# A four-layer graph network on one core: residual adds with row sums on VectorE, variances by ScalarE squares, and an order table that models the DMA queue

## The chip, the core and the metric

The kernel runs on one core of one Trainium2 chip. The core has five engines with an instruction list each: TensorE (PE, matrix products into PSUM), VectorE (DVE), ScalarE (ACT), GpSimd (POOL) and SyncE (SP, which issues DMAs). Each engine takes its instructions strictly in the order of its list and waits on semaphores for the others. DMAs are issued by SP, ACT or POOL and run by themselves. The metric is the device time of one execution in microseconds (us); smaller is better.

## What is computed

The input x holds 16 graphs of 1024 nodes with 256 features, adj is one 1024 x 1024 adjacency matrix. Four layers follow, each of the form x = x + layer(relu(layernorm(x))):

```
h = jnp.maximum(_layernorm(x, axis=-1), 0.0)
x = x + _L0_gnn_ref(h, adj, L0_gnn_W, L0_gnn_a)     # 1 head, leaky_relu 0.01, relu
h = jnp.maximum(_layernorm(x, axis=-1), 0.0)
x = x + _L1_gnn_ref(h, adj, L1_gnn_W, L1_gnn_a)     # 1 head, leaky_relu 0.2, elu
h = jnp.maximum(_layernorm(x, axis=-1), 0.0)
x = x + _L2_gnn_ref(h, adj, ...)                    # dot-product attention, 8 heads, feed-forward
h = jnp.maximum(_layernorm(x, axis=-1), 0.0)
x = x + _L3_gnn_ref(h, adj, L3_gnn_W, L3_gnn_a)     # 4 heads, leaky_relu 0.2, elu
```

Layers 0, 1 and 3 are graph attention: weights exp(leaky_relu(e_src + e_dst)), masked by adj and normalised by row, times the projected features. Layer 2 is masked dot-product attention, whose middle is

```
x = _layernorm(x + t, ln1_g, ln1_b)
h = jax.nn.relu(jnp.einsum('fnc,cd->fnd', x, w1) + b1)
f_out = jnp.einsum('fnd,dc->fnc', h, w2) + b2
x = _layernorm(x + f_out, ln2_g, ln2_b)
```

So each graph passes six layer norms: one at the entry of each layer and two inside layer 2. Everything is fp32.

## The kernel before

All work is cut into tiles of 128 nodes (8 per graph) by 256 features. A stage is one layer of one graph (64 stages). Stages of different layers and graphs overlap: after a start-up the list of stages repeats layer 2, layer 1, layer 3, layer 0 of neighbouring graphs, so that stages that need much PE run beside those that need much DVE or ACT.

The program is first laid out as a list of operations (`op`, line 790), each with an engine, an estimated cost, a rank, the operations that it follows and the buffers it takes and releases. `play` (line 924) then fixes the order: `forward` walks through model time with the costs and with a delay per engine (`DELAY`, line 752), and at each step `choose` takes, of the operations that could begin within 0.5 us, the one with the smallest number in a table, `RANKS` (line 47, three characters for an operation). The instructions are recorded in that order, which is the order of each engine's list. Neither the costs nor the ranks exist at run time: on the chip only the order, the buffers and the semaphores remain.

The parts that matter here:

- **Norms.** `stats_of` (line 1023): DVE's bn_stats and bn_aggr give mean and variance of a tile, POOL forms (variance + eps)^-0.5 in two instructions (L1034, L1035), with a third (L1037) for layer 2. `way_in` (line 1064) uses it at the entry of each layer, `feed_forward` and `finish` inside layer 2. The normalised tile is then transposed on PE (L1054), copied out by ACT (L1057), and projected on PE (L1061).
- **Layers 0 and 1.** `gat_item`: DVE forms masked weights p (L1318), PE multiplies them with the values (L1335). `gat_out`: reciprocal of the row sum, relu (and exp in layer 1) on ACT, then the residual add: on POOL in layer 0 (L1361), two instructions on DVE in layer 1 (L1372, L1373). The next layer's `way_in` follows tile by tile.
- **Layer 3.** `sources` transposes the source terms (L1250), stores them to DRAM as rows `kept` and loads them back spread over all partitions as `r`; `pair_weights` forms the weights on DVE (L1391); PE multiplies them (L1425) and sums them (L1449).
- **Layer 2.** `dot_item` works on items of 128 keys x 512 queries x 4 heads: scores on PE (L1545), exp on ACT in two halves (L1559), mask on DVE in two halves (L1567), values on PE (L1576). The row sums of the weights need only the sum over keys, so two items are first added by a DMA: `gather` (L1593), issued by POOL, adds the odd item's tile (1 MB) onto the even one's with an accumulating DMA. PE sums the result with four matmuls (L1605). A gather waits for the even item's values and both items' masks. There are 256 gathers, 16 for each graph.
- **Feed-forward.** `dot_out` adds the attention to the tile y on POOL (L1658); `feed_forward` normalises (L1044, L1045), multiplies by w1; `finish` multiplies by w2, adds to y on DVE (L1723), normalises again, adds y to x on POOL (L1738), and calls the next layer's `way_in`.

The planner's model gives the gather a cost of 1.0 on POOL and a fixed delay of 8.0 until its result is there.

Of the kernel before, what the change touches and what calls it, by code (L numbers as in the profile page):

```python
# [28 lines left out]
U8 = mybir.dt.uint8  # L29
# [18 lines left out]
    "##,#M5#IA#&O#H2#2l#M)#'c#Q(#H#$6p#MC#GP##q##c#%-#$X##s##0##U#$0#$,##P##X##Y##1#$-##{#$)#$]#$M#%I#$j#$N#%E#%K#%Y"  # L48
    "##%#%O#%}#&Y#&d#&l#&s#';#'B##W##9#oB##N##B#oP##Z##?##>##[##D#ny##a$7g##`##r##l#$##$$#$8#$*##u##z#$6#$=##}#$(#$;"
    "##b#$V$8-##_##y$8,##d##A$7y##g##o#$'#$u##2#$9#$7#$K#%*##*#$H##]#$.##3#$A##t##v#$E#$F#,;##x##6#$5$%$##'#Q.##T#K9"  # L50
    "#K.#(,#%W#'`#'U#$n#)s#'k#%U#(`##^#%7#$&#$%#$1#$2#$C#$G#$I#$L##<#$?#$[#$4##f#%@#%L#&2#$<#$Q##j#81##w#%D#%Z#%`#Nz"
    "#$Z#$`####$r#&1#%f#%k#$Y#$k#%4#>9#%A#%5#%r#%&#%M#${#%=#&##xD#%{#'u#%a#'q#(:#%z#'t#$i##h#$+#$d#$_#$h#$s#$e#$@#`+"
    "#%?#$>#&B#&%#,R#&Z#[=#%;#$O#$v##i##H#'H#%g#%J#%[#%0#%/#%,#&M$D{#$x#%>#%N#%h#b8$?s#&0#(3#&+#&.#%y#%u#&($4Z#&&#&6"
    "#%b#&$#&)#&'$B+#&_#))#&:#%p#Du#;z#<%#%V##n$H^#$b#$p$3b#$^#T>$3P#$m#%1##(#%T##O#%|##R#$}$GF##-#$U##4##8##K#%.##$"
    "##M#%:#$y#$t#$q##I#$z#%<#$W#%)#%8#=M#%6#%+##/##&##@#$g#$a#%w#-%#-##%R$&s##5$=J#%H#%]#3Q#%i#,V#/+#&5#$l#&h#:-#CG"
    "#:=#%d#$S#$|#%2#%c#%j#%m#&,#%t#$J#$w#%x$?=#%C#)*#%F#%B#%l#$o#&-#(U#%Q#'2#+6#%o#&/#0,$'e#'G#h`##p#0'#%^#&7$Gw##k"
    "#%v$Hv#&F$Ha#&N#'-#&A#&Q#&V#&S#lN#&m#&4#'3#'/#b##':#%q#&a#&*#(l#&w#&{#&z#&9#&<$Hw#%S#(R#y$#(S#'6#&;#&?#&^#lO#&G"
    "#Y}#'X#'0#&W#&I#%X#)D#(?#'+#R0#&[#&L#&P#'J#(+#&H#'1#&R#&|#',#'@#&p#'Q#'r#&k#'Y#&f#'C#(f#'.#'L#(8#(=#'N#&U#;v#;l"
    "$-[#&K#&=#&b#&E#&g#&j#&t#''#%s#&i#&o#(y#'9#(;#6F#(<#&n#'$#'8$H'#'a#'y$4|#'5#&]#')#'s#&}$Bt#'^$7k#'l#'?#'<$C2#'h"
    "#'K#'}#<K#%$#'o##.#(6##C#'W#%(#(%##e#'E#'4#'S#'m#'R#'I#(5#'w#'(#'>#'x#jJ#&y$=Z#<J$:z#'F#'O#'7#%G#{)#&v#'z#)V#>U"  # L60
    "#'n#'_#%n#(&#'p#?/#(0#'M#(.#&J#(/#'j#&`#rr#_c#(F#8j#(q#Mm#(M#Mo#(d#Mn#'&#'%#(##'Z#{g#(*#)a#&8##:#(2#(N#(E#/V#)I"
    "#(B#(A#(C#(4#)]$+r#,e#)M#([#i&#((#()#,t#i'#w/#)c#(t#I2#(J#(Y#]h#(K#(V#)F#(_#Ms#(u#KE$Ea#)-#(c#N+#)S#IC#)b#)`#)g"
    "#)U#(i#)d#*(#8?#(m#(|#).#jZ#)1#(a#)$#LT#)##(g#)u#jQ#)n#)0#*R#(k#)8#)@#)C#(j#(]#({#(@#)R#']#)E#(Z#(n#'{#'A#(^#)T"
    "#)>#)G#(P#)&#)5#)v#*&#'P#(G#(X#)y#'D#)L#*q#);#Lj#'|#(9#*3#*$#(D#*,#)K$I0#(O$I@$,q#*##)B#)i#*;#(H#*+#*4#+H#*E#)J"
    "#+L#*9#)A#s}#**#(1#+@#)O#)x#*7#*P#/`#*a#*A#*Z#*8#VE#)?#*D#*0#*y#*6#-0#)N#*_#*k#+k#*s#*C#*^#b($$C#)=#*c#)t#*v#J2"
    "#*[#(w#*w#+U#*I#*i#zG#'v$>>#B=#*]#*g$J:#,h$%D#W5#*n#*M#+<#*|$B<#++#*O#WG#+/#*J#.'#+G$J;#+M#+?#*f#z}#*t#a)#*r$?%"
    "#+A#+8#*j#*u$3:#*d#*p#+d#+a#*S#,U#+C#)+#*-#+`#)}#+&#*K#/?#+R#CO#+O#+P#*}#+[#*'$*M#+^#+S#-[#+X#+c#),#0>#)4#)9#,$"
    "#'*#,v#+N#,r#,W#-<#,N#[S#,x#,O#-:#+D#-A#-G#,B#,d#-(#,j#-;#,L#--#+z#-C#,z#'[#-6#,i#-D#/b#[@#-I#.^#-a$EU#.J#.%$;%"
    "#-}#+b#-j#g)#.:#.)$9j#.7#.?#+B#+F#-H#+(#,&#R+#,D#,%#^1#+#$(u$%|#+)#(Q#-Z#,|#)Y#Lh#*>#2n#+g#+J#*1#cw#)X#,T#+T#,g"
    "#.&#,y#,l#+3#*)#,Z#+e#(-#+>#cj#,'#(L#-2#,5#,)#g`#,6#,:#,4#+}#,##C(#,Q#($$1`#+Z#,9#,X$5H#*L#)W$1_#,Y#-s#,0#+o#,b"  # L70
    "#|5#*B#,}#+r#,s#,?#,@#,>#+u#,n#,8$5J$=r#,K#+]#-Q#+n#.,#-?#.;#,J#+j#+p$5Q#)P#.<$5K#,f#+i#,M#,G#)%#+{#,1#,H#rc#+l"
    "$5P#,3#,S#zA#):#,I$Ab#,c#,/$En#.4$02#*F#,`#,u#,7#-9#+V#-e#,*#-c#.=#-v#-^#-@#-o#-Y#+q#-3#-K#-n#-p#.I#+f#.H#JZ#kE"
    "#,m#.P#.U#,k#.T#-|#.o#/(#k3#.V#.Y#-r#.b#.d#/3#,[#.*#-U#.t#.g#.s#.]#/1#-E#.R#.w#.W#.v#.n#,P#+.#-L#,+#-h#ho#/f#/P"
    "#-5#.k#/O#,]#,-#/Q#0r#/K#/)#/^#8/#-t#8M#-x#-w#/W#-l#)f#(s#)l#)[#*l#+4#)m#*N#*m#)o#+'#%'#)e$<.#*.#)w#*:#*<$Eg$,p"
    "#it#*`#*T#(x#*b#*U#(z$GW#)r#*/#*%#)z#(I#*Y#){#,(#)Q#)|#+I#*e#(>#)Z#*V#*X#)<#*x#*h#W6#+%#+7#`p#+*#+5#`s#+-#+9#^*"
    "#+0$%f#*=#.N#-'#-&#-)#+y#-,#-1#,a#-/#-4#-7#-]#z6#-J$;&#,_#-f#-d#.D#-$#-P#&C$;5#+:#.6#+=#-`#-i#-q#.3#J[#/d#0y#0U"
    "#.M#rQ#B3#.@#-B#,o#.K#,{#0n#._#?V#-g#-z#/t#,.#.9#.e#.G#/Y#.E#.h#/>#-k#./#.L#-F#.+#.8#.A#-X#.C#/0#-=#-{#/'#8-#.["
# [281 lines left out]
    "$Fz$IH$J-$HT$Ib$79#Ul$I?$J5$I+$G|$Iu#hA$EL$Hp$HW$H?$GV$I/$.{$HD#`j$Ig$H_$H:$78#<0#V>$J.$Hs$Ho$Du$HG#GJ$I.$Hu$H|"  # L359
    "#1Z$3G$Hf$HS#_;$HL$Hg$IW#('#y'#<E#xi$I_$J*#M{$J#$I1$J1$GR$I|#<x$II$GO$I($IS#WD$IX$Ia$IV$I]$IB#UX#UW$IT$@<$Im$I="  # L360
    "#q^$IG$IU$IQ$Id$IO#^r$IM#>M$Iz$HI$2d$CB#>e$Iy#yW$It$I}#p4#TS$J?$0R#pU$IZ$Ie$Ij$HN$I:$J@$Hq$Hm$Ih$IP$IL$Ip$I$#:["
    "$I,$IN#5e$I'$If$IY#Y&$Hy#m_$J6#%P$J%#jY$Il#k;#al$J8#wr$I{$J'$J9$Ir$I>"
)


# [1585 lines left out]
```

## Time and profile before

| | |
|---|---|
| Three runs | 4347.82, 4347.32, 4344.05 us; median 4347.32 |
| Profiled execution | 4346.76 us, of which the span from first to last instruction 4344.9 us |
| Mean granted PE clock | 0.983 of full speed |
| Gathers (POOL's DMA queue) | 268.45 MB, 30.7% of the 16 DMA engines' time |
| Exponentials of layer 2, L1559 on ACT | 1024, 1023 ns each |
| Masks of layer 2, L1567 on DVE | 1024, 1233 ns each |
| bn_stats on x, L1030 on DVE | 512, 415 ns each |
| Normalising activation, L1107 on ACT | 256, 505 ns each |
| POOL adds L1361, L1738, L1658 | 128 of 787, 128 of 920, 64 of 1413 ns |
| POOL's root, L1034 and L1035 | 768 of 367 and 768 of 736 ns |

A row of the profile's groups reads: line, engine, operation, output <- inputs by the program's names, their shapes, count, then busy time in us, the mean of one in ns, the idle time of the engine in front of them, and what ended it. A row of waits reads: engine, output and line <- what it waited for: total us, times, longest. Rows of windows give for a stretch of time the busy time of each engine (with its number of instructions), the granted PE clock, the share of the DMA engines and GB/s.

### The profile page before, as it was taken

How to read it: one execution, taken by the hardware profiler on the slowest of the kernel's cores; microseconds unless marked ns; L12 is line 12 of the kernel's file. 1: busy time of each engine (PE TensorE's matmuls, PEld its weight loads, DVE VectorE, ACT ScalarE, POOL GpSimd, SP SyncE). 2: the span in 40 equal slices, each digit the busy share in tenths (PEclk: the TensorE clock that was granted, in tenths of full speed). 3: DMA queues.
4: the chain of work that ended last, by engine and by line, in shares of the span. 5: the costliest groups of instructions: out<-in, count | busy, mean ns of one | idle time of the engine just before them, and what ended most of it. 6: DMA issues, size and time to landing. Idle time of an engine off the chain costs nothing. (4 is left out here: it accounts for less than half of the span.)

```text
span 4344.9 us, 66664 instructions
## 1 busy us (share of the span) xinstructions
PE 4143.8 (95%) x25993; PEld 2175.8 (50%) x25993; DVE 3368.5 (78%) x5836; ACT 2004.2 (46%) x3083; POOL 1408.4 (32%) x2281
## 2 busy tenths in 40 slices
PE   8999999998999999999999999998999999899988
PEld 7735264553645535455354554535545355464433
DVE  7578877878777788777878778777787877858788
ACT  4462635435354453634536354363543635455442
POOL 3323242423324233242322424224242241434231
PEclk9999999999999999999999999999999999999999
DMA  3061805317053170531606235162350713435261
GB/s 111 17 142 32 169 27 117 69 50 155 25 119 79 40 148 26 129 71 46 140 26 141 59 75 111 37 130 59 74 112 33 150 42 89 96 75 111 64 122 41
DMA packets 96451, 364.29 MB, mean 84 GB/s; under 512 B 10376, under 2 KB 45568, under 8 KB 63360
## 3 DMA queue, kind: packets, MB, share of 16 engines
q0 software_dynamic: 36864, 268.45, 30.7%
q1 hardware_dynamic: 58848, 90.98, 6.2%
q8 instruction: 206, 3.38, 0.3%
q14 instruction: 117, 0.96, 0.1%
q10 hardware_dynamic: 416, 0.52, 0.0%
HBM read 74.32 MB, written 17.17 MB: 21 GB/s over the span
## 5 line engine op out<-in xcount | busy, mean ns | idle before, releaser
L1567 DVE TENSOR_TENSOR pe<-pe,mask 128x1024 f32<-128x1024 f32 x1024 | 1206.9, 1233 | 190.5 <-ACT pe L1559 188.3
L1559 ACT ACTIVATE pe<-sc 128x1024 f32<-128x1024 f32 x1024 | 995.4, 1023 | 369.7 <-PE sc L1545 313.8
L1335 PE MATMUL av<-v,p 128*128 128x257 f32 x4096 | 966.8, 387 | 8.5 <-DVE p L1318 6.1
L1335 PEld LDWEIGHTS av<-v,p 128*128 128x128 f32 x4096 | 771.1, 192 | 202.2 <-issue 62.0
L1391 DVE SCALAR_TENSOR_TENSOR p<-r,e,mask 128x1024 f32<-128x1024 f32 x512 | 621.9, 1274 | 95.7 <-DMA r<-kept 85.8
L1545 PE MATMUL sc<-qT,kT 32*128 32x512 f32 x4096 | 626.3, 645 | 2.5 <-ACT pe L1559 2.5
L1035 POOL TENSOR_TENSOR rstd<-rstd,minus_half 128x1 f32<-128x1 f32 x768 | 565.5, 736 | 64.0
L1576 PE MATMUL acc<-pe,v 128*32 128x512 f32 x4096 | 543.0, 605 | 6.1 <-DVE pe L1567 4.7
L1593 POOL DMA_DIRECT2D pe<-pe x256 | 225.6, 888 | 976.8 <-PE acc L1576 669.5
L1034 POOL TENSOR_SCALAR rstd<-stats 128x1 f32<-128x1 f32 x768 | 281.8, 367 | 789.5 <-DVE stats L1031 765.3
L1425 PE MATMUL acc<-p,v 128*32 128x512 f32 x4096 | 465.9, 593 | 0.0
L1605 PE MATMUL sums<-pe,pick 128*32 128x512 f32 x2048 | 294.6, 637 | 127.2 <-DMA pe<-pe 126.4
L1545 PEld LDWEIGHTS sc<-qT,kT 32*128 32x128 f32 x4096 | 192.6, 184 | 388.8 <-issue 184.4
L1061 PE MATMUL pm<-l_wx,hT 128*128 128x259 f32 (+1 forms) x1536 | 369.5, 389 | 2.4 <-ACT hT L1057 1.4
L1318 DVE SCALAR_TENSOR_TENSOR p<-r,e,mask 128x512 f32<-128x512 f32 x512 | 359.2, 755 | 6.8 <-DMA r<-kept 6.4
L1061 PEld LDWEIGHTS pm<-l_wx,hT 128*128 128x128 f32 x1536 | 287.4, 191 | 73.1 <-ACT hT L1057 12.8
L1361 POOL TENSOR_TENSOR x<-x,o 128x256 f32<-128x256 f32 x128 | 100.6, 787 | 570.4 <-ACT o L1357 570.1
L1425 PEld LDWEIGHTS acc<-p,v 128*32 128x32 f32 x4096 | 132.1, 110 | 293.1 <-issue 277.4
L1576 PEld LDWEIGHTS acc<-pe,v 128*32 128x32 f32 x4096 | 100.6, 109 | 353.0 <-issue 223.9
L1030 DVE BATCH_NORM_STATS2 st<-x 128x6 f32<-128x256 f32 x512 | 212.4, 415 | 62.7 <-POOL x L1361 51.3
L1107 ACT ACTIVATE xn<-x,stats 128x256 f32<-128x256 f32 x256 | 124.7, 505 | 291.4 <-DVE stats L1031 235.1
L1449 PE MATMUL sums<-p,e 128*32 128x512 f32 x2048 | 247.5, 593 | 0.3 <-DVE p L1391 0.3
(106 smaller groups left out, 3920.5 us busy)
## 6 DMA issues: line engine op xcount, KB each, us to landing
pe<-pe POOLq DMA_DIRECT2D x256, 1024.0 KB, 8.1
r<-kept SPq DMA_DIRECT2D x64, 512.0 KB
x<-in_x_dram SPq DMA_DIRECT2D x32, 512.0 KB
out_dram<-x SPq DMA_DIRECT2D x64, 256.0 KB
r<-kept SPq DMA_DIRECT2D x62, 256.0 KB
edges<-in_adj_dram SPq DMA_DIRECT2D x8, 512.0 KB
kept<-rows_sb SPq DMA_DIRECT2D x128, 2.0 KB
qkv_sb<-in_L_gnn_w_qkv_dram SPq DMA_DIRECT2D x1, 768.0 KB
```

Of the source, the lines that this page charges most:

```text
L1034: nc.gpsimd.tensor_scalar(rh.t, mh.t[:, 1:2], EPS, None, ALU.add)
L1035: nc.gpsimd.tensor_tensor(rh.t, rh.t, minus_half, ALU.pow)
L1061: nc.tensor.matmul(dst, lhsT=lhsT[:, k, :], rhs=rhs[:, k, :], start=(k == 0), stop=(k == KC - 1))
L1318: nc.vector.scalar_tensor_tensor(ph.t[:, j % each, :], rh.t, s.e[:, j, H + h : H + h + 1], mask[:, j, cols], ALU.max, ALU.mult)
L1335: nc.tensor.matmul(avh.t[:, : s.hs + 1], lhsT=phs[part].t[:, j % each, i * P : (i + 1) * P], rhs=s.v[:, j, h, :], start=(j == 0), stop=(j ...
L1391: nc.vector.scalar_tensor_tensor(ph.t[:, hh, :], s.rh[hp].t[:, hh, :], s.e[:, j, col : col + 1], mask[:, j, :], ALU.max, ALU.mult)
L1425: nc.tensor.matmul(acc[n].t[(2 * hh + part) * W : (2 * hh + part + 1) * W, :], lhsT=s.v[:, jj, h, part * W : (part + 1) * W], rhs=p, start ...
L1545: nc.tensor.matmul(scs[pair].t[:, hh, :], lhsT=s.kh.t[r0 : r0 + D2, g, j * P : (j + 1) * P], rhs=s.qh.t[r0 : r0 + D2, g, cols], start=True ...
L1559: lambda pair=pair: nc.scalar.activation(part(pair), scs[pair].t, AF.Exp, scale=SCALE2),
L1567: lambda pair=pair: nc.vector.tensor_tensor(part(pair), part(pair), masks(), ALU.mult), [ex], tiles=True,
L1576: nc.tensor.matmul(head(acc, i), lhsT=s.v[:, j, g * QUAD + i, :D2], rhs=ph.t[:, i, :], start=(j == 0), stop=(j == NT - 1))
L1605: nc.tensor.matmul(head(sums, i), lhsT=pick[:, g, :], rhs=th.t[:, i, :], start=first, stop=last)
```

## The change

Five edits, all in `fast_path`, and a new order table:

- Two residual adds move from POOL to DVE as one instruction that also gives each row's sum (`accum_out`): layer 0's (`gat_out`), and that of y to x at the end of layer 2 (`finish`). Layer 1's second instruction now gives the sum too.
- The add of the attention to y (`dot_out`) moves from POOL to DVE.
- The add of the feed-forward product to y (`finish`) was one DVE instruction for two tiles and is now one for each tile, with row sums.
- The norms at the entries of layers 1, 2 and 3 and the last norm of layer 2 no longer use bn_stats. `moments_of`: POOL multiplies the row sum by -1/256 (minus the mean), ACT squares the tile with that as its bias and sums the squares (`accum_out`) into a scratch place that is overwritten later, POOL forms the root with 1/256 and eps. The entry of layer 0 and the first norm inside layer 2 keep bn_stats.
- The planner's model has a sixth engine, QUEUE, for the gathers' DMA: the issue on POOL costs 0.9, the transfer 5.2 on QUEUE with a delay of 1.4. No instruction belongs to it.

```diff
-        PE, DVE, ACT, POOL, SP = range(5)
+        PE, DVE, ACT, POOL, SP, QUEUE = range(6)
 
-        DELAY = (0.2, 0.12, 0.14, 0.06, 2.0)
+        DELAY = (0.2, 0.12, 0.14, 0.06, 2.0, 1.4)
...
-        def affine(y, m, r, g, b):
-            nc.vector.scalar_tensor_tensor(y, y, m, g, ALU.subtract, ALU.mult)
+        def moments_of(src, scratch, mh, rank, after, shift=False, takes=(), ends=()):
+
+            rh = buffer(small, "rstd", (P, 1), "rstd")
+
+            def square():
+                nc.scalar.activation(scratch(), src(), AF.Square, bias=mh.t[:, 0:1], accum_out=mh.t[:, 1:2])
+
+            def root():
+                nc.gpsimd.tensor_scalar(rh.t, mh.t[:, 1:2], 1.0 / C, EPS, ALU.mult, ALU.add)
+                nc.gpsimd.tensor_tensor(rh.t, rh.t, minus_half, ALU.pow)
+                if shift:
+                    nc.gpsimd.tensor_scalar(mh.t[:, 1:2], mh.t[:, 0:1], rh.t, None, ALU.mult)
+
+            m_op = op(
+                POOL, 0.25, rank,
+                lambda: nc.gpsimd.tensor_scalar(mh.t[:, 0:1], mh.t[:, 2:3], -1.0 / C, None, ALU.mult), after,
+            )
+            q_op = op(ACT, 0.45, rank + 0.4, square, [m_op], takes=[rh, *takes], ends=ends)
+            r_op = op(POOL, 1.15 if shift else 0.85, rank + 1.0, root, [q_op], ends=[mh])
+            return q_op, r_op, rh
...
-        def way_in(s, t, rank, after):
+        def way_in(s, t, rank, after, mh=None):
...
+            if L == 0:
+                m_op, r_op, mh, rh = stats_of(xt, rank, after)
+                takes = takes + ([xnh] if i == 0 else [])
+            else:
+                m_op, r_op, rh = moments_of(
+                    xt, src, mh, rank, after + s.began, shift=L == 2,
+                    takes=([s.yh] if t == 0 else []) if L == 2 else ([xnh] if i == 0 else []),
+                )
...
-                add = op(POOL, 0.7, rank + 0.9, lambda: nc.gpsimd.tensor_add(xt(), xt(), oh.t), [o], ends=[oh], tiles=True)
+                add = op(
+                    DVE, 0.4, rank + 0.9,
+                    lambda: nc.vector.scalar_tensor_tensor(
+                        xt(), oh.t, 1.0, xt(), ALU.mult, ALU.add, accum_out=mh.t[:, 2:3]
+                    ), [o], takes=[mh], ends=[oh], tiles=True,
+                )
...
-                    nc.vector.scalar_tensor_tensor(xt(), oh.t, -1.0, xt(), ALU.add, ALU.add)
+                    nc.vector.scalar_tensor_tensor(
+                        xt(), oh.t, -1.0, xt(), ALU.add, ALU.add, accum_out=mh.t[:, 2:3]
+                    )
...
-            gathered = op(POOL, 1.0, at[0] - 4.0, gather, [valued] + ready + masked, ends=[ph], delay=8.0)
+            issued = op(POOL, 0.9, at[0] - 4.0, gather, [valued] + ready + masked, delay=0.6)
+            gathered = op(QUEUE, 5.2, at[0] - 4.0, lambda: None, [issued], ends=[ph])
...
-                    nc.gpsimd.tensor_add(yt, yt, zh.t.rearrange("p (t c) -> p t c", t=TH))
+                    nc.vector.tensor_add(yt, yt, zh.t.rearrange("p (t c) -> p t c", t=TH))
...
-                def add(t=n * TH + 2 * u, u=u):
-                    y2 = s.y[:, t : t + 2, :]
-                    nc.vector.tensor_add(y2, y2, pmh.t[:, u].rearrange("p (u c) -> p u c", u=2))
+                def add(t=n * TH + 2 * u, u=u, mhs=mhs):
+                    for i, mh in enumerate(mhs):
+                        yt = s.y[:, t + i, :]
+                        nc.vector.scalar_tensor_tensor(
+                            yt, yt, 1.0, pmh.t[:, u, i * C : (i + 1) * C], ALU.mult, ALU.add, accum_out=mh.t[:, 2:3]
+                        )
...
-                        POOL, 0.7, at + 3.0, lambda xt=xt, yt=yt: nc.gpsimd.tensor_add(xt(), xt(), yt()), [normed],
-                        ends=[s.yh], tiles=True,
+                        DVE, 0.4, at + 3.0,
+                        lambda xt=xt, yt=yt, nh=nh: nc.vector.scalar_tensor_tensor(
+                            xt(), yt(), 1.0, xt(), ALU.mult, ALU.add, accum_out=nh.t[:, 2:3]
+                        ), [normed], takes=[nh], ends=[s.yh], tiles=True,
```

The table `RANKS` is replaced as a whole (the operations are more in number), so the order of every engine's list changes, PE's too; the matmuls themselves are the same.

## The prediction

> **What bounds the kernel now.** I read the page's busy shares first, then who TensorE (PE) waited for, then PE's own instructions around one long wait, then the granted clock there.
>
> ```profile
> PE 4143.8 (95%) x25993; PEld 2175.8 (50%) x25993; DVE 3368.5 (78%) x5836; ACT 2004.2 (46%) x3083; POOL 1408.4 (32%) x2281
> ```
>
> PE is the bound: everything that can be won lies in its 201.0 us of idle time (span 4344.9 less 4143.8) and in matmuls that ran slowly. The other engines matter only where PE waits for them. The list of PE's waits:
>
> ```profile
> PE sums L1605 <- DMA pe<-pe: 126.4, 64, 6.7
> PE tp L1054 <- ACT xn L1107: 11.9, 5, 7.5
> PE pm L1061 <- ACT hT L1057: 11.0, 11, 1.2
> PE count L1909 <- DVE broken L1907: 7.2, 1, 7.2
> PE tp L1054 <- DVE y L1045: 6.2, 12, 1.7
> ```
>
> Two thirds of the idle time is one wait: the row sums of the attention weights (L1605) wait for the accumulating DMA that adds one weight tile to another (the "gather", issued by POOL at L1593). All other PE waits are 58 us together, 7.2 of them the check at the very end. PE around such a wait (start, length, instruction, idle time before it):
>
> ```profile
> 1600.94 1.10 PE L1605 MATMUL sums<-pe,pick 128*32 128x512 f32 x6
> 1606.99 1.93 PE L1605 MATMUL sums<-pe,pick 128*32 128x512 f32 x8 [4.95 <-DMA pe<-pe]
> 1608.86 3.52 PE L1335 MATMUL av<-v,p 128*128 128x257 f32 x8
> 1612.30 1.06 PE L1605 MATMUL sums<-pe,pick 128*32 128x512 f32 x8
> 1616.77 1.94 PE L1605 MATMUL sums<-pe,pick 128*32 128x512 f32 x8 [3.40 <-DMA pe<-pe]
> ```
>
> The waits come in clusters, where several gathers were issued close together. And the wait costs twice: behind it the same eight matmuls take 1.93 us instead of 1.06. The clock column (PEclk) says why:
>
> ```profile
> 1606.00:1612.00 6.00, 5.01 (x16) 2.72 (x16) 5.69 (x14) 0.51 (x1) 3.23 (x5) 0.50 1.06 217
> 1640.00:1646.00 6.00, 6.00 (x21) 3.77 (x20) 5.25 (x16) 3.18 (x6) 3.16 (x8) 1.00 0.00 0
> ```
>
> The trace's clock records hold 28 stretches at 0.50, 151 us in all, PE busy in 110 of them; at half speed that lost 55 us. Some 41 of the 55 are in stretches that begin behind a wait for a gather.
>
> **The gather, and the order around it.** A gather's time from issue to landing is 6.9 us at best, 8.1 in the median, 17.8 at most; landings behind each other in a burst are 4.8 to 5.1 us apart. So a gather issued alone lands in 7 us, and one issued in a burst queues. To see what the new order does I count on the two built programs' instruction lists. Each PE instruction gets its row's busy time over its count (av 0.236 us, sc 0.153, and so on); these add up to 4405 us, more than the 4143.8 busy, because neighbours overlap, so all are scaled by 0.941. Then for every one of the 256 gathers: it can leave once the even item's values (L1576) are done and 4.0 us after the odd item's scores (two exponentials of 1.02, one mask multiply of 1.23, hops); the issue takes 0.9; it lands 6.1 later, and no sooner than 4.9 after the gather before it. Its sums are late if their place in PE's list comes earlier. For the order before, this count gives 128.8 us of lateness in 40 places; the trace has 126.4 in 64. That is near enough to trust the count. For the new order it gives 12.4 us in 14 places, none over 2.3. Places with less than 9 us of PE work between a gather's last input and its sums fall from 71 to 62, those under 8 from 28 to 16: the sums were moved back where gathers crowd.
>
> The count leaves out POOL's own queue. With POOL's instructions kept in their order as well, 42 gathers of the new order stand behind a POOL instruction that is not ready (75 us of standing in all; before, 46 and 100 us), and the lateness becomes 27 to 30 us. I take 20, between the two: **-106 us** (ends -122 and -96).
>
> **Clock.** With waits of at most 2.3 us most half-speed stretches should go; gaps of 1.4 to 2.2 us have set off three of the 28, so not all. Of the 41 us I take back 36: **-36 us** (ends -10, if short waits keep the clock low, and -45). [...]
>
> **Engine work that moves.** Per run, VectorE (DVE) loses 512 statistics pairs (bn_stats 0.415 or 0.409, aggregate 0.182: 304 us) and the 64 two-tile residual adds (0.676: 43). It gains 128 layer-0 adds and 128 closing adds (128x256, 0.46 each: 118), 128 residual adds from PSUM (0.44: 56), 64 adds of 128x512 (0.70: 45) and 512 accumulator reads (0.08: 41). Net -87 us, DVE from 3368 to about 3280. I credit nothing for it, since PE does not wait for DVE in sum; it covers DVE in a shorter span (78% still). What an accumulating add costs can be read in the weights' set-up:
>
> ```profile
> L689 DVE SCALAR_TENSOR_TENSOR scr<-l_wx,rows_in 128x256 f32<-128x256 f32 x12 | 4.8, 462 | 0.0
> L689 DVE DVE_READ_ACCUMULATOR scr<-l_wx,rows_in 128x1 f32 x36 | 2.9, 80 | 0.0
> L1373 DVE SCALAR_TENSOR_TENSOR x<-o,x 128x256 f32<-128x256 f32 x128 | 61.0, 477 | 14.0 <-DVE x L1372 0.5
> ```
>
> Accumulating (462) costs no more than not (477), plus an 80 ns read. [...]
>
> ACT gains 512 Squares of 128x256. The nearest row is the normalising activation L1107, 505 ns, so 259 us; an accumulator read on ACT is not in the trace, between nothing and the 264 ns of a 128x3 activation (0 to 135 us; I take 40, by DVE's 80 ns). ACT goes to about 2300 us, 54%. Behind a waiting Square on ACT stand exponentials (L1559), for which DVE's masks and PE's values wait. POOL loses 320 adds (306 us) and gains 512 one-column multiplies by -1/256 (0.367, 188 us): -118. Behind a waiting multiply on POOL stand roots and gathers.
>
> **The norm chain gets longer.** From sum to normalised tile it was bn_stats and aggregate (0.60) and the root; now an accumulator read (0.08), a POOL multiply (0.37), a Square (0.50), the root: +0.35, with two more hops some +0.55 us. PE sees it only at its 160 transposes of rows (L1054), of which 17 wait now (11.9 + 6.2 us). The place of these transposes in the new list leaves them about as much PE work as before. Ends: 0 if every chain has that slack, 88 us if none has (160 x 0.55). I take 18 late chains, **+10 us**, near today's 17.
>
> **Sources of layer 3.** In the trace the first weights (L1391) start 8.0 to 8.8 us after the transpose L1250 in 14 of 16 stages: copy, eight stores, load. The old list keeps at least 12.0 us of PE work between that transpose and the first use; the new one 3.4 us in batch 15, the very last stage, and 8.5 in batch 0. First weights are there 8.3 + 1.3 = 9.6 us after: 6.2 and 1.1 us late, with a little for the weights that follow at DVE's pace: **+9 us** (ends 6 and 14). Before, the load was covered by the previous pair's values; that cover is gone.
>
> **Sum.** 4344.9 - 106 - 36 + 10 + 9 = 4222 us span; the profiled execution's time lies 1.9 above its span, and the median of the runs 0.6 above it: **4224 us**. Its own range: best ends 4344.9 - 122 - 45 + 0 + 6 + 2.5 = 4186; worst 4344.9 - 96 - 10 + 88 + 14 + 2.5 = 4343, which needs every term bad at once; two of the three large ones half way to bad (-23 us of clock, +49 of chains) give 4276.
>
> **Rivals.**
> 1. *Gathers later than counted, part of the gain lost.* If every gather of the new order is ready d later than counted (ACT's Squares and POOL's multiplies ahead of it), the count gives 37 us at d = 1, 93 at 2. At 2: 4344.9 - 33 - 11 of clock + 19 + 2.5 = 4322. For it: 512 more POOL and ACT instructions that wait for each other. Against: fewer gathers stand blocked, and POOL has 118 us less to do.
> 2. *The same past its turning point: slower.* Place: POOL's in-order queue at L1593. The count passes the old 126.4 at d = 2.4, and gives 195 us at 3: 4344.9 + 69 + 22 of clock + 19 + 2.5 = 4457. It decides from d = 2.2 on. Against: POOL's multiplies and roots are 0.2 to 0.9 us each, and 2.2 us for all 256 gathers is three such in front of each one.
> [...]
> 4. *The DMA wait was not the cause, and PE waits elsewhere instead* (for DVE, whose work by 100 us of PE work reaches 0.95 in both orders, 1.04 before and 1.08 now in the last layer 3): gains fall to the clock's few us, 4335 to 4350.
>
> **Chances.** Forecast 0.72, rival 1 0.12, rival 2 0.08, rival 3 0.04, rival 4 0.04. Runs spread over 0.09%, so 0.2% (9 us) is about what can be told from no change. Faster by more: 0.72 + 0.12 + 0.04 and a part of rival 4, 0.89; within 0.03; slower 0.08. The range reaches from 4180 to 4295, leaving out part of rival 1 and all of 2 and 4.
>
> **What would show it.** Right: PE's wait for the gather falls from 126 to 10-40 us, no wait of it over 4 us; the mean clock rises from 0.983 to above 0.99; PE's busy time falls to about 4105 though it does the same matmuls; DVE near 3280, ACT near 2300 with one table load, POOL near 1290; a new PE wait of some 6 us for L1449 or L1425 near the end. Wrong: PE waiting for tp (L1054 before) or for exponentials by tens of us, gathers landing later than 10 us in the median, or Squares that take much more than 0.55 us.

## The result, and the profile after

The kernel after takes 4214.39 us (median of 4 runs, 4212.81 to 4219.8) beside 4345.89 us for the kernel before (4 runs on the same chip). The ratio is 0.970, with a 95% interval of 0.9683 to 0.9716: 3% faster, and 10 us under the forecast of 4224. The profiled execution has a span of 4212.7 us.

The first line of the page of the kernel after (busy us, share of the span, instructions):

```profile
PE 4106.9 (97%) x25993; PEld 2166.0 (51%) x25993; DVE 3202.1 (76%) x5708; ACT 2272.0 (54%) x4107; POOL 1291.4 (31%) x2473
```

PE does the same 25,993 matmuls in 36.9 us less, and is still the bound. DVE lost 166 us, ACT gained 268, POOL lost 117. What PE waits for (us in all, times, longest), in the kernel after:

```profile
PE sums L1667 <- DMA pe<-pe: 38.3, 40, 2.7
PE tp L1099 <- ACT xn L1160: 9.5, 5, 7.7
PE count L1980 <- DVE broken L1978: 7.2, 1, 7.2
PE sums L1510 <- DVE p L1452: 6.0, 2, 5.6
PE pm L1106 <- ACT hT L1102: 5.5, 6, 1.2
PE av L1388 <- ACT o L1411: 4.3, 8, 1.6
```

The wait for the gather (the first line) went from 126.4 us in 64 places to 38.3 in 40, and its longest from 6.7 to 2.7. The fourth line is new: the first sums of a layer-3 stage wait 5.6 us at 4151 us, in the last stage, for weights whose sources were loaded late. All waits of PE over 0.15 us together, from its first instruction on: 184.2 us before, 87.5 after. (The first wait, from the start of the span, is left out of these sums: 7.5 us before and 7.7 after. It is the 7.7 in the second line.)

One of the gather waits that are left, and what stands behind it, in PE's timeline (start, length, instruction, idle time before it):

```profile
1563.01 1.36 PE L1637 MATMUL acc<-pe,v 128*32 128x512 f32 x6
1566.63 1.06 PE L1667 MATMUL sums<-pe,pick 128*32 128x512 f32 x8 [2.26 <-DMA pe<-pe]
1567.63 5.43 PE L1388 MATMUL av<-v,p 128*128 128x257 f32 x16
```

Sixteen matmuls of values take 5.43 us here. At their row's mean they would take 16 x 0.232 = 3.7 us (950.9 us over 4096). The stretches of time before and around them (us, busy time of PE, PEld, DVE, ACT, POOL, granted clock, DMA share, GB/s) show the reason:

```profile
1564.50:1567.91 3.41, 1.28 (x9) 0.44 (x10) 3.41 (x8) 1.61 (x4) 2.30 (x4) 1.00 0.89 180
1567.91:1571.33 3.42, 3.42 (x9) 2.70 (x9) 3.28 (x9) 1.11 (x3) 0.50 (x2) 0.50 0.66 134
```

The granted clock is 1.00 in the first, into which the wait of 2.26 us falls, and 0.50 in the second. The clock records hold 8 half-speed stretches (39.3 us, PE busy in 24.3) where before they held 28 (151.2 us, PE busy in 110.1). At half of PE's busy time in them, half speed costs 12 us now, and cost 55.

The records also say when a stretch comes. All eight begin on one grid of 3.413 us (to within 6 ns); six last one period, one lasts two, and the last runs on past the end. What precedes them is a period in which PE was idle for about half of the time or more: of the periods at full clock in this trace, all 7 in which PE was busy for less than half were followed by half speed, 1 of the 7 between 0.5 and 0.6, and none of the 1205 above. In the kernel before it was 25 of 30, 2 of 10 and 1 of 1183. So in these two traces a stretch goes with how much idle time falls into one such period, and not with the length of a single wait alone. This is read off the traces; no run varied it.

So the 132.2 us by which the span fell are, by the two traces:

| part | before | after | difference | as predicted |
|---|---|---|---|---|
| PE waits for gathers | 126.4 | 38.3 | -88.1 | -106 |
| PE busy (of it lost to half speed: 55, then 12) | 4143.8 | 4106.9 | -36.9 | -36 |
| PE waits for layer 3's sources | 0.3 | 6.0 | +5.7 | +9 |
| all other PE waits over 0.15 us | 57.5 | 43.2 | -14.3 | +10 |
| the two ends of the span and gaps under 0.15 us | 16.9 | 18.3 | +1.4 | 0 |
| sum (span) | 4344.9 | 4212.7 | -132.2 | -123 |

The last row of parts is what is left of the span after the four above it. Two parts came out other than forecast, 18 us worse and 24 us better, and these two cancel: that the time came within 10 us of the forecast is to that extent luck.

Rows of the operations that moved, in the kernel after (busy us, mean ns of one, idle time before):

```profile
L1072 ACT ACTIVATE xn<-x,stats 128x256 f32<-128x256 f32 x256 | 129.2, 505 | 114.5 <-POOL stats L1082 113.6
L1072 ACT ACTIVATION_READ_ACCUMULATOR xn<-x,stats 128x1 f32 x256 | 48.7, 190 | 0.0
L1432 DVE SCALAR_TENSOR_TENSOR x<-o,x 128x256 f32<-128x256 f32 x128 | 54.5, 426 | 13.7 <-DVE x L1431 0.9
L1432 DVE DVE_READ_ACCUMULATOR x<-o,x 128x1 f32 x128 | 10.5, 82 | 0.0
```

A Square takes 505 ns, as its neighbour row said, and a read of ACT's accumulator 190 ns, in the middle of its bounds. An adding instruction with a row sum takes 426 ns and its read 82, where the rows in the prediction had 462 and 80.

### The profile page after: what moved, and what is told of

It reads as the page before. It is cut to its first block, busy times and chain, and to the rows that moved or that the text cites. A ratio compares the mean times of both kernels' runs of the same rounds, so it can differ in the third digit from the quotient of the medians.

```text
span 4212.7 us, 67513 instructions
## 1 busy us (share of the span) xinstructions
PE 4106.9 (97%) x25993; PEld 2166.0 (51%) x25993; DVE 3202.1 (76%) x5708; ACT 2272.0 (54%) x4107; POOL 1291.4 (31%) x2473
## 4 chain that ended last, share of the span: by engine, by line
PE 76%; DMA 7%; DVE 6%; issue 5%; ACT 3%; POOL 2%; POOLq 0%; ACTq 0%; SPq 0%; DVEq 0%
PE pm L1106 20%; PE av L1388 19%; PE acc L1486 11%; PE sc L1606 7%; DMA pe<-pe 7%; PE acc L1637 6%; PE sums L1510 5%; PE tp L1099 3%; DVE pe L1628 3%; PE sums L1667 3%; ACT pe L1620 1%; POOL rstd L1076 1%; PE tpv L1549 1%; PE tpo L1686 1%; POOL pe L1654 1%
## 5 line engine op out<-in xcount | busy, mean ns | idle before, releaser
L1388 PE MATMUL av<-v,p 128*128 128x257 f32 x4096 | 950.9, 382 | 6.9 <-ACT o L1411 4.3
L1388 PEld LDWEIGHTS av<-v,p 128*128 128x128 f32 x4096 | 760.6, 190 | 194.1 <-issue 56.1
L1082 POOL TENSOR_SCALAR stats<-stats 128x1 f32<-128x1 f32 x512 | 166.4, 333 | 886.0 <-DVE x L1417 564.2
L1076 POOL TENSOR_TENSOR rstd<-rstd,minus_half 128x1 f32<-128x1 f32 x512 | 353.4, 690 | 42.7
L1667 PE MATMUL sums<-pe,pick 128*32 128x512 f32 x2048 | 272.5, 600 | 39.0 <-DMA pe<-pe 38.3
L1075 POOL TENSOR_SCALAR rstd<-stats 128x1 f32<-128x1 f32 x512 | 175.0, 342 | 275.6 <-ACT xn L1072 143.3
L1055 POOL TENSOR_SCALAR rstd<-stats 128x1 f32<-128x1 f32 x256 | 94.2, 368 | 478.3 <-DVE stats L1052 472.5
L1106 PE MATMUL pm<-hT,qkv_sb 128*128 128x512 f32 x512 | 231.1, 597 | 2.3 <-ACT hT L1102 2.3
```

The source lines that it names most:

```text
L1076: nc.gpsimd.tensor_tensor(rh.t, rh.t, minus_half, ALU.pow)
L1106: nc.tensor.matmul(dst, lhsT=lhsT[:, k, :], rhs=rhs[:, k, :], start=(k == 0), stop=(k == KC - 1))
L1388: nc.tensor.matmul(avh.t[:, : s.hs + 1], lhsT=phs[part].t[:, j % each, i * P : (i + 1) * P], rhs=s.v[:, j, h, :], start=(j == 0), stop=(j ...
L1667: nc.tensor.matmul(head(sums, i), lhsT=pick[:, g, :], rhs=th.t[:, i, :], start=first, stop=last)
```

## The experiments

**What is to be told apart.** The prediction put the gain down to PE's new order and credited the moved engine work with nothing. So theory 1: the order carries the gain, and the engines only have to keep up. Theory 2: the moved work makes room that the order needs, and neither is worth much alone. A third question was whether what is left of the gather wait is the DMA queue.

### The new order's rank table with the old engines

All moved operations go back to the engines of before, in the plan too; the new rank table and the new model of the gather stay.

```diff
-            q_op = op(ACT, 0.45, rank + 0.4, square, [m_op], takes=[rh, *takes], ends=ends)
+            q_op = op(DVE, 0.54, rank + 0.4, stats, [m_op], takes=[rh, mh, *takes], ends=ends)
...
-                add = op(DVE, 0.4, rank + 0.9, ...accum_out=mh.t[:, 2:3]), [o], takes=[mh], ends=[oh], tiles=True)
+                add = op(POOL, 0.7, rank + 0.9, lambda: nc.gpsimd.tensor_add(xt(), xt(), oh.t), [o], ends=[oh], tiles=True)
...
-                    DVE, 0.65, rank + 2.6 + g, add, ...
+                    POOL, 1.35, rank + 2.6 + g, add, ...
```

> The new order table and the planner's DMA queue kept, every moved operation put back: bn_stats in all six norms, the adds of layer 0, of the attention and of the closing on POOL, one two-tile add on DVE. The count on this kernel's instruction lists gives 35 us of late gathers (after: 12, before: 129). Theory A, the order of PE's list does it: PE's wait for the gathers falls to 35-75 us, most of the clock loss goes, 4240-4270 us. Theory B, the moved operations do it (POOL freed, so gathers leave earlier): the wait stays above 100 us, 4310-4350 us.

Measured: 4588.61 us, ratio 1.055 (1.0534 to 1.0572): slower than the kernel before by 245 us. What PE waits for in this kernel:

```profile
PE acc L1629 <- DVE pe L1620: 78.8, 17, 16.1
PE acc L1478 <- DVE p L1444: 70.8, 23, 10.8
PE sums L1659 <- DMA pe<-pe: 48.7, 42, 3.8
```

The gathers are waited for little longer than in the kernel after (48.7 us, 38.3 there). But PE now waits 149.6 us for DVE's masked weights (the two acc lines), up to 16 us at a time, which neither kernel does. A rank table holds one number for each operation; with other costs and engines the planner plays it into another list.

### The old ranks with the new engines

The reverse: the operations of the kernel after, each with the rank that its counterpart had in the kernel before, and the gather planned as before.

```diff
 RANKS = (
-    "#n9##*##2$J[##)#K}#Mm##0##-#$M$6G$>S$IB#$7##z###$+x#$S##4##w#%+#$I#$:##n##$#$(#$t#$B#$'#%c#$^#*>#%}#$d#'%#&;#gR"
...
+    "##-#P*#Ky#&^#Jb#3n#Ov#'w#T)#JP$=}#P9#Iz##s##e#%1#$]##u##1##W#$2#$.##R##Z##[##2#$/##}#$+#$a#$P#%Q#$n#$Q#%M#%S#%c##%"
...
-            issued = op(POOL, 0.9, at[0] - 4.0, gather, [valued] + ready + masked, delay=0.6)
-            gathered = op(QUEUE, 5.2, at[0] - 4.0, lambda: None, [issued], ends=[ph])
+            issued = op(POOL, 1.0, at[0] - 4.0, gather, [valued] + ready + masked, delay=0.0)
+            gathered = op(QUEUE, 0.0, at[0] - 4.0, lambda: None, [issued], ends=[ph], delay=8.0)
```

> The reverse: the operations on their new engines, but every operation takes its rank from the table of before (a Square that of the bn_stats it replaces) and the gather has its old cost and fixed delay in the planner. The count gives 106 us of late gathers. Theory A: PE waits for the gathers 105-165 us, 4320-4390 us. Theory B: the wait falls under 70 us, 4240-4280 us.

Measured: 4555.96 us, ratio 1.048 (1.0462 to 1.0504). PE's waits in this kernel:

```profile
PE sums L1658 <- DMA pe<-pe: 99.1, 66, 4.4
PE acc L1477 <- DVE p L1443: 44.1, 13, 10.0
PE tp L1090 <- ACT xn L1151: 34.2, 26, 7.4
```

The gather wait is back (99.1 us in 66 places; 126.4 in 64 before), so it does go with the order. But both mixtures lose 210 to 245 us against the kernel before. Most of it are waits that belong to neither parent; PE's busy time is longer too, by 77 to 80 us. These two runs tell where the gather wait comes from; on what the moves are worth they say nothing, since each also got a list that nobody had chosen. That needs a list that is held fixed (below).

### Gathers that leave later

Two one-column power operations on POOL before every gather. The expectation took them at 0.7 us each; in the trace they take 1.04 us in the mean.

```diff
+                for _ in range(2):
+                    nc.gpsimd.tensor_tensor(lag, lag, minus_half, ALU.pow)
                 nc.gpsimd.dma_start(
```

> The changed kernel with two 0.7 us POOL instructions on a spare column in front of every gather, some 1.5 us later each, PE's list unchanged. If the count of lateness by d holds from its zero (12 us at 0), the wait becomes about 62 us and the time 4214 + 24 + 10 of clock = about 4250. If the measured 38 us mean that gathers already come 1 us later than counted, the wait becomes about 140 us and the time 4214 + 102 + 35 = about 4350, and the first rival of the prediction is real at this price.

Measured: 4268.41 us, ratio 0.982 (0.9799 to 0.9839), 54 us more than the kernel after. PE's wait for gathers here:

```profile
PE sums L1671 <- DMA pe<-pe: 61.2, 53, 4.9
```

The wait rose by 22.9 us and the half-speed stretches from 8 to 15 (PE busy in 56.2 us of them, 24.3 in the kernel after, so 16 us more lost). The rest of the 54 us, some 15, are other short waits and a longer busy time of PE. The 61.2 us agree with the count's 62, but only by chance: the count is too low by 8 to 26 us for the kernel after itself, and the two operations depend on nothing, so where POOL stood waiting anyway they delayed no gather. By the times of the instructions in the two traces, the issue of a gather begins 1.44 us behind its last input here and 0.67 us in the kernel after (means of the 256). What is shown is the price of rival 1: some 0.8 us of delay in front of the gathers cost 54 us, well short of the 131 that would make the change a loss.

### Gathers a quarter as long

Each gather adds only the first quarter of its tile (256 KB for 1 MB). The row sums of three heads in four then lack the odd items.

```diff
-                    out=th.t.rearrange("p i q -> p (i q)"), in_=ph.t.rearrange("p i q -> p (i q)"), accum_op=ALU.add
+                    out=th.t.rearrange("p i q -> p (i q)")[:, :HALF],
+                    in_=ph.t.rearrange("p i q -> p (i q)")[:, :HALF], accum_op=ALU.add,
```

> The changed kernel with gathers that add only the first head's quarter of the odd item's tile (256 KB instead of 1 MB), so row sums of three of four heads lack the odd items. If the queue's service time is what is left of the wait: landing falls from 8.4 to 3-4 us, PE's wait for gathers to under 3 us, no half-speed stretches behind them, time 4214 - 36 - 8 = about 4170. If the left-over waits are POOL's own lateness, the wait stays above 15 us and the time above 4190.

Measured: 4178.29 us, ratio 0.961 (0.9592 to 0.9631), 36 us under the kernel after. The rows of the gather's DMA (KB each, median us from issue to landing), first in the kernel after:

```profile
pe<-pe POOLq DMA_DIRECT2D x256, 1024.0 KB, 8.4
```

and then in this kernel:

```profile
pe<-pe POOLq DMA_DIRECT2D x256, 256.0 KB, 3.3
```

No wait of PE for a gather is left. The issue and all that goes before it are as they were. So the 38 us that are left in the kernel after need the transfer's own time and its queue; whatever Squares and multiplies delay the issue does not reach PE by itself. The 36 us are a net gain: other waits of PE rose by 13 us in their place. The half-speed stretches hardly changed (7, PE busy in 22.5 us of them), so the 8 us of clock that the expectation had counted on did not come, and the time stayed 8 us above it.

The trace of the kernel after tells the two causes of a late gather apart. The issues of the 40 late ones began 0.33 us (median, 0.50 in the mean, over 1 us in four cases) behind their last input, as those of all gathers do: they were not held up on POOL. But 32 of the 40 stood behind another gather in the queue. From the landing of that one, such a gather took 4.9 to 9.0 us, 5.9 in the mean (all 179 that queued: 5.5), where the count had 4.9. An estimate from the two traces: with every issue where the trace has it and PE's times held, the count's rule for landings leaves 5 us of lateness in the kernel after, where the landings themselves give 37. In the kernel before it leaves 62, where the landings give 124.

### The list held fixed, the old engines in it

For these three the planner's operations, costs and ranks are those of the kernel after, so that PE's list and the place of every operation are kept. Only the function that an operation carries out is given back to the old engine. First the statistics alone: bn_stats and its aggregate on DVE, at the place where ACT's Square stood.

```diff
             def square():
-                nc.scalar.activation(scratch(), src(), AF.Square, bias=mh.t[:, 0:1], accum_out=mh.t[:, 1:2])
+                st = small.tile([P, 6], F32, tag="bn", name="st", bufs=3)
+                nc.vector.bn_stats(st, src())
+                nc.vector.bn_aggr(mh.t[:, 0:2], st)
```

> The planner's list, costs and ranks are those of the kernel after, so PE's order is the same instruction for instruction. Only the engine that works out the four norms' variances goes back: bn_stats and bn_aggr on VectorE at the place where ScalarE's Square stood; the adds stay on VectorE without row sums. VectorE: 3202.1 + 512 x (0.415 + 0.182) - 512 x 0.08 = some 3467 us; ScalarE: 2272 less 512 x (0.505 + 0.19) = some 1917. Theory 1 (the new order of PE carries the gain, the engines only have to keep up): 4205 to 4235, PE's wait of the sums for gathers stays at 30 to 45 us, no new wait over 15 us. Theory 2 (the order fits only the loads of the engines that it was found with): over 4260, with new waits of PE for VectorE's products (weights, masks) of 40 us or more, although no instruction of PE's has moved.

Then the statistics and the adds on POOL:

```diff
-                    lambda: nc.vector.scalar_tensor_tensor(
-                        xt(), oh.t, 1.0, xt(), ALU.mult, ALU.add, accum_out=mh.t[:, 2:3]
-                    ), [o], takes=[mh], ends=[oh], tiles=True,
+                    lambda: nc.gpsimd.tensor_add(xt(), xt(), oh.t), [o], takes=[mh], ends=[oh], tiles=True,
...
-                    nc.vector.tensor_add(yt, yt, zh.t.rearrange("p (t c) -> p t c", t=TH))
+                    nc.gpsimd.tensor_add(yt, yt, zh.t.rearrange("p (t c) -> p t c", t=TH))
```

> As the run before it, and the layer-0, attention and closing residual adds are back on GpSimd too, at the places where VectorE did them in the list: GpSimd some 1291 + 128 x 0.787 + 128 x 0.92 + 64 x 1.41 - 512 x 0.367 = 1412 us, VectorE back to some 3300. PE's order is still that of the kernel after. Theory 1: 4205 to 4240, gather waits 30 to 50 us. Theory 2: the adds take 0.4 to 0.7 us longer each inside a chain from values to normalised rows, and gathers stand behind them on GpSimd: 4270 or more, waits of PE's transposes and of its sums both up by 20 us or more.

And the kernel after with the attention add alone on POOL (the last two lines of that diff):

> The kernel after, with the attention output's add alone back on GpSimd (64 adds, 1.413 us there by the trace before, some 0.70 on VectorE). Same order of PE. Theory 1: within 10 us of the kernel after (4204 to 4224). Theory 2: each of the 64 adds delays its chain by 0.7 us and a hop, and what is behind it on GpSimd (gathers) by 1.4: at most 64 x 0.9 = 58 us if every chain is on the path, and then 4230 to 4270.

Measured, on one chip (before: 4342.41 us there). The last row, and the profiles of the first and last, are from the first measurement:

| kernel | us | ratio, interval | PE waits | of it gathers | lost to half speed |
|---|---|---|---|---|---|
| before | 4342.4 | 1 | 184.2 | 126.4 | 55 |
| list of after, all old engines | 4313.9 | 0.994 (0.9923 to 0.9954) | 153.2 | 37.0 | 19 |
| list of after, old statistics | 4274.4 | 0.984 (0.9826 to 0.9856) | 129.7 | 38.2 | 23 |
| list of after, old attention add | 4249.6 | 0.978 (0.9763 to 0.9795) | 106.0 | 39.1 | 19 |
| after | 4214.4 | 0.970 (0.9683 to 0.9716) | 87.5 | 38.3 | 12 |

Theory 1 falls: the order alone, with the old engines, gains 0.6% and not 3%. The list is the same, matmul by matmul, in the last four rows, and the wait for gathers is 37 to 39 us in every one of them, so that part does belong to the order. With the old engines it is paid back in many short waits. What PE waits for with all old engines:

```profile
PE sums L1667 <- DMA pe<-pe: 37.0, 39, 3.3
PE tp L1101 <- DVE y L1092: 22.4, 27, 2.3
PE tp L1101 <- ACT xn L1162: 18.8, 14, 7.5
PE av L1390 <- ACT o L1413: 16.7, 17, 2.8
PE tp L1101 <- DVE xn L1155: 10.5, 11, 1.5
```

and with the attention add alone on POOL:

```profile
PE sums L1667 <- DMA pe<-pe: 39.1, 41, 3.9
PE tp L1099 <- DVE y L1090: 12.1, 17, 1.9
```

The transposes of normalised rows (tp) wait for the chain that leads to them; in the kernel after they wait 0.9 us for DVE's y, here 22.4 and 12.1. Theory 2 has the direction, but not its mechanism: not masks and weights are late above all (9.5 us with all old engines, for masks), but the norm chains: all waits of these transposes rise by 39 of the 66 us by which PE's waits rise.

For the attention add the chain is shown. On POOL it takes 1.32 us instead of 0.69 on DVE (L1720 in the two kernels, 64 each), and from the scaling of the attention to the end of the add it takes 3.0 us instead of 1.9 in the mean. The 64 cost 35 us together, 0.55 us each.

For the Squares only the price is shown. With the old statistics alone PE waits:

```profile
PE tp L1101 <- ACT xn L1162: 18.7, 15, 7.3
PE av L1390 <- ACT o L1413: 16.7, 15, 3.1
```

The kernel after has 9.5 and 4.3 us there. All waits rise by 42 us, and PE's busy time by 21, of which half speed explains 11. DVE is busy 3443.3 us in that run, 241 more. Counted by instructions the chain with bn_stats is the shorter one, and in the trace it is not longer everywhere: from the residual add to the normalised tile 5.2 us instead of 5.0 at the entry of layer 1 and 6.3 instead of 6.5 at that of layer 2, and 12.0 instead of 11.0 around the last norm of layer 2 (means). That work stands in DVE's fuller list is the likely cause, but no run changes DVE's load without the chain.

Of the fall from before to after, the list is worth some 29 to 32 us by this path, the adds some 39, the Squares some 60. This is one path through the mixtures; a list found for other engines would give other shares, and the list of before, held fixed with the new engines, was not run. Of the 28 us by which PE's busy time is longer with all old engines (4134.5 less 4106.9) half speed explains 7; the rest stays open.

### Sums set later in PE's list

If the gather wait is queue time, PE could do other work meanwhile. In the kernel after, 60 groups of sums are moved behind one to six of the PE groups that follow them.

```diff
+            LATER = {661: 683, 707: 1092, 722: 834, 737: 849, 909: 940, 924: 1114,
...
+            for late, passed in sorted(LATER.items()):
+                i = next(i for i, x in enumerate(best[1]) if x[2].number == late)
+                x = best[1].pop(i)
+                j = next(j for j, y in enumerate(best[1]) if y[2].number == passed)
+                assert j >= i
+                best[1].insert(j + 1, x)
```

> The kernel after, with 60 groups of row sums of the weights set later in PE's list, each past one to six other groups of PE's, where the count of gathers (landing 4.9 us behind each other, 1.5 us of delay taken on) has them late. Nothing else moves. By that count the lateness at a delay of 1.5 us goes from some 105 to 9 us. Theory (what is left of the gather wait is time in the DMA queue, and PE can do other work meanwhile): the wait of 38.3 us goes under 12, a part of the 12 us that half speed still costs goes too, 4172 to 4192; the run with the short gather, 4178, is about the floor. Rival (the sums held up nothing but themselves, and later sums hold the weights' buffers longer): exponentials wait for buffers, PE waits for exponentials instead, 4205 to 4225.

Measured: 4236.24 us, ratio 0.976 (0.9748 to 0.9775): 22 us slower than the kernel after. The largest of PE's waits in this kernel, but for the transposes of the first rows:

```profile
PE tps L1703 <- ACT sums_sb L1694: 13.4, 19, 0.7
PE av L1405 <- DVE p L1388: 10.0, 13, 1.3
PE sums L1684 <- DMA pe<-pe: 9.6, 15, 2.0
PE av L1405 <- ACT o L1428: 9.2, 11, 1.6
```

The gather wait did fall to 9.6 us, as the theory said, but not the time. All waits together rose from 87.5 to 94.5. The transposes of the sums (tps) now stand right behind the sums, with a copy between (13.4 us, 2.0 before), and the values that were pulled forward wait for their weights (10.0 us, 1.1 before) and for ACT to free their places (9.2 us, 4.3 before). PE's busy time rose too, by 13.6 us, although half speed cost 6 us less; the scores alone rose by 13.1. Their row in the kernel after, and then in this one:

```profile
L1606 PE MATMUL sc<-qT,kT 32*128 32x512 f32 x4096 | 634.0, 641 | 2.7 <-ACT pe L1620 1.2 <-ACT pm L1072 0.6 <-ACT kT L1274 0.2
```

```profile
L1623 PE MATMUL sc<-qT,kT 32*128 32x512 f32 x4096 | 647.1, 640 | 7.7 <-ACT pe L1637 3.6 <-DVE turned L1730 1.8 <-ACT pm L1089 0.6
```

The mean of one is the same, but they overlap less: runs of 16 score matmuls in a row (3.4 us, where two runs of 8 take 1.14 us each) went from 8 to 16, since the sums that kept them apart were moved away. That is some 9 of the 13 us. Neither theory had this. The time lies 11 us above the rival's range (4205 to 4225), and its mechanism (exponentials waiting for buffers) gave 3.6 us only.

### A list that is searched, not shifted

A place in the list has to be weighed as a whole. So single operations in the lists of PE, DVE and ACT were moved one to eight places wherever the planner's own play of the lists got shorter. The kernel after then takes the list that came out.

```diff
+            digits = [DIGITS.index(c) for c in LIST]
+            played = {x[2].number: x for x in best[1]}
+            best[1][:] = [played[(x * 90 + y) * 90 + z] for x, y, z in zip(digits[::3], digits[1::3], digits[2::3])]
             for ring, places in best[2].items():
```

> The kernel after with the same operations, engines and buffers, and lists of PE, VectorE and ScalarE searched further: single operations were moved one to eight places earlier or later wherever that shortened the planner's own play of the lists (its costs, a gather 5.2 us in the queue; 5.7 us, and 3% more on VectorE and ScalarE, counted too). 856 of PE's places hold another operation than before. The planner's play of the kernel after ends at 4220.7 us (the chip's span was 4212.7); of the run with the later sums it says 46 us more (the chip 20 more span), of this list 33 less. Theory (what keeps PE idle is still the order, and the planner's model of it is good enough to search with): half to all of the 33 us, 4180 to 4200. Rival (the search has fitted itself to the model; real engines differ from its costs by more than the gain): 4205 to 4230.

Measured: 4204.74 us (4204.02 to 4205.55), ratio 0.968 (0.9668 to 0.9695). That is 10 us under the kernel after, less than a third of the 33 that the model gave, and between the ranges of the theory and the rival. PE's busy time fell by 15.6 us (to 4091.3) and its waits rose by 8.4 (to 95.9), though the gathers' part fell to 26.9.

The kernel after once more, and a list searched as long again, on one chip:

> The kernel after, unchanged, beside the next run on the same chip: what it takes here is the yardstick for the searched list. 4205 to 4222.

> The searched list of the run before, searched as long again, GpSimd's list too (the gathers in their order). The planner's play of it ends 8 us earlier than that of the list before (4180.1 against 4187.8), with a gather of 5.6 us in the queue some 12. Theory (the order is still what can be improved, at a third to half of what the model says, as the run before had it): 4194 to 4204, 10 to 20 us under the kernel after on the same chip. Rival (the search follows the model, not the chip): no better than the list before it, 4202 to 4212.

Measured: the kernel after 4213.91 us, ratio 0.9704 (0.969 to 0.9718); the list searched further 4210.84 us, ratio 0.9699 (0.9686 to 0.9712). The second search gained nothing; the rival was right on it. Two of its waits:

```profile
PE sums L2008 <- DMA pe<-pe: 24.9, 31, 2.7
PE tp_mask L2216 <- DVE flags L2210: 11.8, 1, 11.8
```

The second line is PE's very first work in this list. In the kernel after eight transposes of rows stand before it, at 7.7 us, and it waits 1.6 us behind them; PE is idle for 11.8 us at the start here and for 9.4 there. The first searched list lies 0.2% under the kernel after, but the intervals of the ratios overlap a little (0.9668 to 0.9695 and 0.969 to 0.9718) and the two were measured apart: likely better, not settled.

## Why the prediction was right, step by step

- **Gather waits, -106 (measured -88).** The mechanism was right: the longest wait was to be under 4 us and is 2.7, and the wait follows the order in every mixture. The size was off by 18 us. The term that was too small is "lands 6.1 later, and no sooner than 4.9 after the gather before it": the late gathers that queued took 5.9 us in the mean, and this rule leaves 5 us of lateness by the trace's own issue times where 37 came. That the count gave 128.8 us for the kernel before, near the 126.4 measured, was partly luck: by the issue times of that trace the rule gives half. The quarter-size gather shows that without the transfer's length nothing is left of the wait.
- **Clock, -36 (measured -37 in PE's busy time).** Right in its direction, and a little lucky in its size: half speed lost 55 us and loses 12, which is -43, and the rest of PE's busy time rose by 6. Not counting on every short wait being free was right: no gather wait is over 2.72 us any more, and still stretches of half speed begin at 479 us behind a wait of 2.72, at 1568 behind 2.26, and at 3343 behind 1.69. The stretches begin on a grid of 3.413 us, and PE need not be idle through the whole of the period before one: it was busy for 32, 38 and 51% of the period before these three. The prediction had gone by the length of single waits.
- **Engine work that moves, credited with nothing.** The sizes were near: DVE 3202 us (forecast 3280), ACT 2272 (2300), POOL 1291 (1290). The reason given, that PE does not wait for DVE in sum, was wrong. With the same list and the old engines the kernel takes 4314 us, so the moves are worth 100 us in this list. With the old engines PE does wait for what DVE and POOL make, often and shortly, in an order that leaves the norm chains less room. For the attention add that is shown; for the Squares, the largest part, the mechanism stays open. That was hidden in the forecast, because order and engines came together and the sum charged only for what is late in the new pair.
- **Norm chain, +10 (measured: PE's waits at transposes 18.1 before, 15.2 after, -3; 7.5 and 7.7 of these are the first wait of the span).** The sign was wrong, as far as two different lists can tell. The step was "two more hops some +0.55 us" in place of the statistics, with 18 late chains; it left out that three of the adds ahead of the norm moved off POOL, where they took 0.79, 0.92 and 1.41 us, onto DVE, where the first two take 0.42 and the third 0.69. The 35 us of the attention add alone show the size of what I left out. PE's waits before products (pm) fell too, 15.8 to 8.4 us.
- **Layer 3's sources, +9 (measured +5.7).** Right in its place, the last stage, and in its 6.2 us there (5.6). Batch 0 showed nothing; its 1.1 us were covered.
- **Rival 1** (gathers ready later) had little part in the result: the late gathers of the kernel after began 0.5 us later than the count had them, by their inputs in the trace. The count's 37 us for a delay of 1 us is near the 38.3 measured, but for another reason. Its price was measured: 54 us for two short operations ahead of each gather. **Rival 2** would have needed 2.2 us of delay, where the late gathers began 0.5 us later than counted.
- **Rival 3** (accumulating adds that take longer) is refuted by the rows themselves; no run shows such an add. Accumulating adds take 417 to 426 ns in the kernel after. The same instructions without a row sum, in the run with the old statistics, take 408 to 426. For the second add of layer 1, there:

```profile
L1434 DVE SCALAR_TENSOR_TENSOR x<-o,x 128x256 f32<-128x256 f32 x128 | 54.5, 426 | 14.0 <-DVE x L1433 0.9
```

  So the sum costs at most its read of 82 ns, and that runs beside its neighbours: all 564 reads together make DVE's busy time 1.6 us longer.
- **Rival 4** (PE waits for DVE's products instead) came true only where the list did not fit the engines: 149.6 us in the first mixture; in the kernel after 1.9 us for the masks.

## What to carry to other kernels

An order table and the placement of work on engines are one solution: judge a move with the list held fixed, because with the list played anew each mixture gets a list of its own, and both of ours were 5% slower than the kernel before. A wait that is taken from PE by setting its work later is only won if what is pulled forward is ready and what is pushed back has nobody close behind it; here 29 us of gather wait were won and 22 us of time lost. And price a queued transfer by the mean it takes behind another one (5.5 us here), not by the best cases (4.9).

## What was not expected of the hardware

- POOL's 32 copies of 128x8 (L1288) have a mean of 1293 ns in the kernel after, where the same line (L1235) had 360 before. The line's own view (shortest/median/longest ns, first and last start) takes that back:

```profile
L1288 POOL COPY v<-e x32: 191/198/29778, 26.3 to 3769.1; 128x8 f32<-128x8 f32 x32
```

  The median is 198 ns; one of the 32 is recorded as 29.8 us and makes the mean. It is the sixth of them. It is no accident of one run: the mean of this line is 1275 ns in the run with late gathers, 1292 with all old engines in the fixed list and 1294 with the attention add alone on POOL. What held it was not tried; nothing in PE's waits goes back to it.
- A read of ACT's accumulator is an instruction of its own, 188 to 194 ns behind each Square, more than twice DVE's 82. The 512 of them are 97.6 us, but they run mostly beside their neighbours: ACT's busy time is 35 us longer for them.
- Squares needed no table load beyond the one of 1283 ns that the kernel before has too.
- In both traces half speed comes in periods of 3.413 us on a fixed grid (8 stretches after, 28 before). PE was busy for 53% or less of the period before each of them, but for one in the kernel before (76%). Waits of 1.7 to 2.7 us were enough for three of the eight.
